# One table of places: the pieces of a two-layer graph attention kernel put in another order

## The chip, the cores and the metric

The kernel runs on one core of a Trainium2 chip. The metric is the device time of one execution in microseconds (us). Three executions of the kernel before took 2467.41, 2478.37 and 2482.59 us, so its median is 2478.37 us. The profile used here is of one more execution, whose span from the first to the last instruction is 2471.9 us, with a mean granted TensorE clock of 0.997. All data is fp32.

## The reference

There are 128 graphs of 128 nodes with 512 features, and one adjacency matrix for all. Two layers follow each other.

```python
# layer 0: scores weighted by the adjacency, divided by their norm, no softmax
q, k, v = x @ Wq.T, x @ Wk.T, x @ Wv.T
rel = adjacency.T * (q @ k.T)
rel = rel / norm(rel, axis=2)
x = layernorm(x + rel @ v)
# layer 1: attention with 8 heads of 64 features, masked where adj == 0
q, k, v = x @ Wq + bq, x @ Wk + bk, x @ Wv + bv
weights = softmax(q @ k.T / sqrt(64) + mask)        # per head
x = layernorm(x + weights @ v)
```

## The kernel before

**Rounds.** The 128 graphs are worked in 32 rounds of 4 graphs (`NG = 32`, `G = 4`). A round has five projections, called `m` (layer 0, query and key weights folded into one matrix), `v0`, `q`, `k` and `v1`. Each is done by a two-level scheme that replaces matrix products by sums. Its pieces are `inner` (line 458: two or four products of 128x128 by 128x128) and `whole` (line 503: two products of 128x128 by 128x256).

**Layer 0.** `l0_score` (line 544, four 128-column products of a graph), `l0_norm` (line 558: the column sums of the squares, as products of 32 columns of the array, tile `pn`), `l0_out` (line 594, one 512-column product), `l0_layernorm`.

**Layer 1, for each graph b = 0 to 3.** `attn_scores` (line 611) makes eight products, one for each head, that contract over 64 rows only (tile `ps`, line 617). VectorE adds the mask and finds the maxima (`masked`, line 129), 16 instructions a graph. `attn_exp` (line 633) is on ScalarE, two heads a piece. Then the weights are transposed with the help of DRAM: `attn_spill` (line 640) writes them out, `attn_stage` (line 646) reads them back in another arrangement into the tile `wl`, of which there is one, and `attn_transpose` (line 654) is one VectorE instruction over 128x1024 elements. `attn_out` (line 661) makes eight products that fill 64 columns of the array (tile `po`, line 669). `attn_back` and `attn_rows` send the result through DRAM again, `attn_res` fetches the residual, `attn_sum` adds (VectorE line 701, GpSimd lines 703 and 705), and `attn_stats`, `attn_norm` and `attn_write` finish the graph. The last round does its attention in another form (`last_...`).

**Weights.** Of each projection's weights a part stays on the chip and a part (896 KB) is fetched each round by `stream` (line 191) into a ring of two tiles named `wr`.

**What sets the order.** Nothing decides the order at run time. Every piece has a place in the table `KEYS` (line 814): five numbers, for round 0, for round 1, for the rounds 2 to 29, for round 30 and for the last round, counted in units of which 35 make a round (`R = 35`). All pieces are sorted by 35 x round + place, and each engine's queue is filled in that order:

```python
    def at(f, g, a, n):
        keys = KEYS[n]
        k = keys[0] if g is None else R * g + keys[0 if g == 0 else 1 if g == 1 else 4 if g == NG - 1 else 3 if g == NG - 2 else 2]
        todo.append((k, len(todo), f, a))
...
    with tc.manual_schedule():
        layer0_weights()
        for _, _, f, a in sorted(todo, key=lambda t: t[:2]):
            f(*a)
```

Each engine takes its own queue in order and waits at its head; SyncE (SP) issues all DMAs, in order too. A place above 35 means that the piece is done while later rounds are under way: graph 2's scores of a round, at 61.65, stand at 26.65 of the next round. Below, places are given within a round, modulo 35.

The short products are these two loops:

```python
        for a in range(H // 2):                      # attn_scores, line 614
            for s in range(2):
                r = slice(s * HD, (s + 1) * HD)
                nc.tensor.matmul(p[s][:, :, a, :], QT[g][r, a, b, :], KT[g][r, a, b, :], start=True, stop=True)
...
        for a in range(H // 2):                      # attn_out, line 666
            for s in range(2):
                h = 2 * a + s
                nc.tensor.matmul(p[s * HD:(s + 1) * HD, a, :], V1[g][b // 2][:, b % 2, h * HD:(h + 1) * HD],
                                 wT[:, s * (H // 2) + a].rearrange("p q t -> p (q t)"), start=True, stop=True)
```

PSUM tiles come from two pools: `ps_m` with six banks (line 53; the scores of a graph take two, the results of `attn_out` one) and `ps_a` with two (line 52).

Of the kernel before, what the change touches and what calls it, by code (L numbers as in the profile page):

```python
# [18 lines left out]
def kernel(  # L19
# [786 lines left out]
    def last_store(g, b):  # L806
# [8 lines left out]
        ("inner", "k", 0, 0): (33.9, 26.7, 31.7, 34.3, 21.3),  # L815
        ("inner", "k", 0, 1): (34.7, 28.4, 34.6, 35.7, 22),
        ("inner", "k", 0, 2): (36, 30.6, 35.74, 37.9, 22.8),
        ("inner", "k", 0, 3): (39, 34.1, 37.5, 39.8, 23.9),
        ("inner", "k", 1, 0): (37, 27.9, 33.04, 35.6, 21.9),
        ("inner", "k", 1, 1): (38.2, 29.3, 33.9, 35.8, 22.7),  # L820
        ("inner", "k", 1, 2): (38.5, 30.7, 35.7, 38.8, 23),
        ("inner", "k", 1, 3): (39.8, 33.2, 37.1, 40, 24),
        ("inner", "m", 0, 0): (None, -48, -24.4, -25.1, -24.6),
        ("inner", "m", 0, 1): (None, -44, -22.46, -21.7, -23),
        ("inner", "m", 0, 2): (None, -40, -20.83, -20, -21.47),
        ("inner", "m", 0, 3): (None, -31.2, -19, -16.2, -19.8),
        ("inner", "m", 1, 0): (None, -43, -23, -23, -24.5),
        ("inner", "m", 1, 1): (None, -39.4, -21.8, -21.8, -21.8),
        ("inner", "m", 1, 2): (None, -32, -20.2, -20.3, -21),
        ("inner", "m", 1, 3): (None, -30, -18.3, -14.4, -18),  # L830
        ("inner", "q", 0, 0): (25.2, 32.3, 27.73, 27.2, 11.2),
        ("inner", "q", 0, 1): (28.7, 32.6, 28.24, 33.4, 13.2),
        ("inner", "q", 0, 2): (30.3, 37, 31.6, 35.46, 16),
        ("inner", "q", 0, 3): (32.3, 38, 32.6, 36, 25.3),
        ("inner", "q", 1, 0): (27.9, 34.7, 27.9, 27.7, 13),
        ("inner", "q", 1, 1): (29.5, 35.97, 29.31, 29.64, 15.97),
        ("inner", "q", 1, 2): (31, 37.7, 31, 31.7, 20.5),
        ("inner", "q", 1, 3): (32.1, 38.7, 32.3, 35.5, 26.3),
        ("inner", "v0", 0, 0): (None, -46, -14.9, -14.1, -16.2),
        ("inner", "v0", 0, 1): (None, -31.4, -13.2, -12.9, -13.2),  # L840
        ("inner", "v0", 0, 2): (None, -27, -12.2, -12.5, -11),
        ("inner", "v0", 0, 3): (None, -24.3, -12, -11.4, -10),
        ("inner", "v0", 1, 0): (None, -39, -14.6, -14.01, -13.8),
        ("inner", "v0", 1, 1): (None, -32.6, -13.07, -12.6, -12.7),
        ("inner", "v0", 1, 2): (None, -26, -12.11, -12, -10.9),
        ("inner", "v0", 1, 3): (None, -22, -11, -11.3, -10.5),
        ("inner", "v1", 0, 0): (38.7, 39.05, 38.4, 41.3, 44),
        ("inner", "v1", 0, 1): (40.4, 41.08, 40.4, 42.6, 46.4),
        ("inner", "v1", 0, 2): (43, 44.89, 41.8, 45.6, 47.8),
        ("inner", "v1", 0, 3): (46.68, 45.5, 44.04, 46.6, 52),  # L850
        ("inner", "v1", 1, 0): (39.7, 39.27, 40.7, 41.6, 45),
        ("inner", "v1", 1, 1): (40.8, 40, 41.9, 45, 49.7),
        ("inner", "v1", 1, 2): (44.2, 44.2, 43.1, 45.4, 58),
        ("inner", "v1", 1, 3): (46.5, 44.8, 43.8, 46.4, 61),
        ("step", "m", 1): (-96, None, None, None, None),
        ("step", "m", 2): (-74, None, None, None, None),
        ("step", "m", 3): (-64, None, None, None, None),
        ("step", "m", 4): (-44, None, None, None, None),
        ("step", "m", 5): (-75, None, None, None, None),
        ("step", "m", 6): (-71, None, None, None, None),  # L860
        ("step", "m", 7): (-63, None, None, None, None),
        ("step", "v0", 1): (-49, None, None, None, None),
        ("step", "v0", 2): (-27, None, None, None, None),
        ("step", "v0", 3): (-28, None, None, None, None),
        ("step", "v0", 4): (-21.3, None, None, None, None),
        ("step", "v0", 5): (-45, None, None, None, None),
        ("step", "v0", 6): (-40, None, None, None, None),
        ("step", "v0", 7): (-31, None, None, None, None),
        ("whole", "k", 1, 0): (38, 34, 35.8, 38.09, 23.8),
        ("whole", "k", 1, 1): (39.2, 35, 37.9, 40.05, 26.5),  # L870
        ("whole", "k", 6, 0): (40.6, 38.1, 40.6, 42.5, 30),
        ("whole", "k", 6, 1): (42, 40.9, 42.3, 44.1, 35),
        ("whole", "k", 7, 0): (44, 42, 43.4, 45.11, 35.6),
        ("whole", "k", 7, 1): (44.1, 43, 44, 45.3, 38),
        ("whole", "m", 1, 0): (None, -39.3, -19.76, -19, -21.4),
        ("whole", "m", 1, 1): (None, -28, -17.6, -14.2, -19),
        ("whole", "m", 6, 0): (None, -25.9, -16.4, -14, -17),
        ("whole", "m", 6, 1): (None, -23, -14, -11.63, -14),
        ("whole", "m", 7, 0): (None, -16.6, -12.8, -11, -12.9),
        ("whole", "m", 7, 1): (None, -13.2, -12.02, -10, -11.7),  # L880
        ("whole", "q", 1, 0): (31.1, 37.4, 33.2, 37, 18),
        ("whole", "q", 1, 1): (38.4, 39.1, 35.6, 38.4, 27.5),
        ("whole", "q", 6, 0): (41, 39.8, 37.6, 39.82, 33),
        ("whole", "q", 6, 1): (42.7, 41.3, 40, 41, 35.5),
        ("whole", "q", 7, 0): (44.5, 44.1, 42.6, 44, 41),
        ("whole", "q", 7, 1): (45, 44.5, 43.2, 45.1, 42.3),
        ("whole", "v0", 1, 0): (None, -24, -10.3, -10.5, -9.99),
        ("whole", "v0", 1, 1): (None, -18, -9.66, -9.8, -9.5),
        ("whole", "v0", 6, 0): (None, -16, -8.9, -8.6, -8),
        ("whole", "v0", 6, 1): (None, -14, -7.28, -7.4, -7.7),  # L890
        ("whole", "v0", 7, 0): (None, -13.14, -6.58, -6.5, -5.4),
        ("whole", "v0", 7, 1): (None, -8, -5.68, -4.06, -5.37),
        ("whole", "v1", 1, 0): (46.7, 46.5, 44.05, 46.7, 56.6),
        ("whole", "v1", 1, 1): (47.7, 48.5, 46.2, 46.9, 60),
        ("whole", "v1", 6, 0): (49, 50.7, 47.6, 49.2, 64.4),
        ("whole", "v1", 6, 1): (50.2, 52.8, 49.4, 51.9, 67.2),
        ("whole", "v1", 7, 0): (50.85, 54, 52.56, 54, 72),
        ("whole", "v1", 7, 1): (53, 54.6, 53.4, 56, 73),
        ("attn_back", 0): (69.5, 67, 68.7, 83.7, None),
        ("attn_back", 1): (64.37, 65.6, 67.94, 92, None),  # L900
        ("attn_back", 2): (74.25, 76, 78.3, 97, None),
        ("attn_back", 3): (82.2, 83.6, 80.2, 63, None),
# [269 lines left out]
```

## Time and profile before

| what | us | share of the span |
|---|---|---|
| TensorE (PE) busy | 2421.0 | 98% |
| VectorE (DVE) busy | 1969.6 | 80% |
| GpSimd (POOL) busy | 1464.7 | 59% |
| ScalarE (ACT) busy | 1031.8 | 42% |
| DMA queue of SP: 549.81 MB | | 77.3% of 16 engines |

Over four rounds in the middle (1223 to 1533 us) the busy times change little from round to round: PE 76.6, 75.2, 76.6 and 75.9 us of 77 or 78 us, and VectorE 61 to 62 us of them. The share of PE is of modelled ends: a matmul's record is longer than the distance to the next one's start (a 128-column product of two records takes 0.223 us from start to start, while each record is 0.275 us long). So the starts are read here and not the lengths.

### The profile page before, as it was taken

The page shows a single profiled execution, that of the slowest core. Times are in us where ns is not written, and L with a number is a line of the kernel's source. Part 1 is how long each engine was busy: PE and PEld are TensorE (multiplying, and loading weights), DVE is VectorE, ACT ScalarE, POOL GpSimd, SP SyncE. Part 2 cuts the span into 40 slices and gives each one's busy share as a digit, 9 for nine tenths or more (in the row PEclk, how much of TensorE's full clock was granted, in tenths as well). Part 3 has the DMA queues.
Part 4 walks back from the last instruction along what each step waited for, and adds up shares of the span by engine and source line. Part 5 has one row for each costly group of instructions (what it writes and reads, how often), then busy time and mean ns, then how long its engine had stood idle before and what let it go on. Part 6 is the DMA issues. An engine that isn't in the chain of part 4 may idle for free.

```text
span 2471.9 us, 54459 instructions
## 1 busy us (share of the span) xinstructions
PE 2421.0 (98%) x18456; PEld 2147.3 (87%) x18456; DVE 1969.6 (80%) x5440; ACT 1031.8 (42%) x3598; POOL 1464.7 (59%) x1958
## 2 busy tenths in 40 slices
PE   8999999999999999999999999999999999999998
PEld 6889888889888888888898888888888988888887
DVE  5678888778888788787887877888887888877887
ACT  1244343444443443434434444444344344344354
POOL 5746655556565566555665555656556656556664
PEclk9999999999999999999999999999999999999999
DMA  8577877878787878778787788887787878787774
GB/s 203 175 200 223 249 221 221 240 211 244 225 229 227 222 226 237 221 221 231 233 244 212 223 232 227 228 235 232 218 232 229 250 220 228 224 233 222 241 224 140
DMA packets 532247, 553.28 MB, mean 224 GB/s; under 512 B 40192, under 2 KB 427392, under 8 KB 531968
## 3 DMA queue, kind: packets, MB, share of 16 engines
q1 hardware_dynamic: 531968, 549.81, 77.3%
q8 instruction: 145, 2.38, 0.4%
q14 instruction: 134, 1.10, 0.2%
HBM read 380.44 MB, written 169.21 MB: 222 GB/s over the span
## 4 chain that ended last, share of the span: by engine, by line
PE 72%; DMA 13%; DVE 5%; SPq 4%; POOL 3%; issue 2%; ACT 0%; DVEq 0%; POOLq 0%
PE pa_v L446 11%; PE pc_v L456 9%; PE pc_q L456 7%; DMA wl<-wd 7%; PE pc_k L456 5%; PE pa_k L446 5%; PE pa_q L446 5%; PE ps L617 4%; PE po L669 4%; PE pa_m L446 4%; PE po L597 4%; PE pc_m L456 4%; PE pst L552 3%; DMA wd<-w 3%; DMA xl_h<-x1d 2%
## 5 line engine op out<-in xcount | busy, mean ns | idle before, releaser
L637 ACT ACTIVATE w<-w,nmax 128x128 f32<-128x128 f32 x992 | 387.3, 396 | 308.6 <-DVE nmax L130 308.5
L446 PE MATMUL pa_v<-wc_v,tx 128*128 128x256 f32 x1024 | 264.6, 386 | 9.3 <-DVE v L501 9.0
L130 DVE CUSTOM_DVE_ANT_0 w<-ps,mask 128x128 f32<-128x128 f32 x1024 | 224.0, 286 | 44.0 <-PE ps L617 42.6
L446 PEld LDWEIGHTS pa_v<-wc_v,tx 128*128 128x128 f32 x1024 | 180.1, 191 | 35.0 <-DVE v L501 13.7
L637 ACT ACTIVATION_READ_ACCUMULATOR w<-w,nmax 128x1 f32 x992 | 191.1, 193 | 0.0
L656 DVE STREAM_TRANSPOSE wT<-wl 128x1024 f32<-128x1024 f32 x124 | 153.1, 1235 | 42.9 <-DMA wl<-wd 42.0
L567 POOL TENSOR_TENSOR rn<-ss,mhalf 128x4 f32<-128x4 f32 x32 | 33.0, 1031 | 207.6 <-DVE ss L565 207.6
L456 PE MATMUL pc_v<-wd_v,ux 128*128 128x128 f32 x756 | 146.3, 275 | 0.1
L456 PE MATMUL pc_v<-wr_v,tx 128*128 128x128 f32 x756 | 146.2, 275 | 0.0
L456 PE MATMUL pc_v<-wr_v,ux 128*128 128x128 f32 x756 | 146.2, 275 | 0.0
L701 DVE TENSOR_TENSOR o<-o,rs 128x512 f32<-128x512 f32 x118 | 126.4, 1075 | 23.3 <-DMA o<-od 23.2
L617 PEld LDWEIGHTS ps<-kT,qT 64*128 64x128 f32 x1984 | 118.2, 187 | 30.1 <-issue 19.9
L669 PE MATMUL po<-wT,v 128*64 128x128 f32 x1984 | 135.7, 279 | 7.1 <-DVE wT L656 6.8
L577 POOL TENSOR_SCALAR ve<-st 128x1 f32<-128x1 f32 (+1 forms) x157 | 35.8, 228 | 177.5 <-DVE st L573 169.6
L617 PE MATMUL ps<-kT,qT 64*128 64x128 f32 x1984 | 136.5, 282 | 0.0
L446 PE MATMUL pa_k<-tx,wc_k 128*128 128x256 f32 x512 | 134.2, 386 | 0.3 <-DVE kT L493 0.3
L446 PE MATMUL pa_q<-tx,wc_q 128*128 128x256 f32 x512 | 134.3, 385 | 0.1
L446 PE MATMUL pa_m<-tx,wc_m 128*128 128x256 f32 x512 | 131.4, 380 | 0.0
L669 PEld LDWEIGHTS po<-wT,v 128*64 128x64 f32 x1984 | 106.1, 136 | 29.1 <-issue 14.2
L456 PEld LDWEIGHTS pc_v<-wd_v,ux 128*128 128x128 f32 x756 | 124.3, 191 | 7.4 <-ACT s_v L475 0.5
L552 PEld LDWEIGHTS pst<-yT,xT 128*128 128x128 f32 x1024 | 125.0, 193 | 3.3
L597 PE MATMUL po<-v,rel 128*128 128x512 f32 x256 | 125.6, 594 | 0.0
(315 smaller groups left out, 7456.5 us busy)
## 6 DMA issues: line engine op xcount, KB each, us to landing
wd<-w SPq DMA_DIRECT2D x248, 256.0 KB, 3.6
wl<-wd SPq DMA_DIRECT2D x496, 128.0 KB, 3.9
wr_v<-wr_v SPq DMA_DIRECT2D x63, 896.0 KB, 6.9
xl_x<-in_x_dram SPq DMA_DIRECT2D x256, 128.0 KB, 3.6
x<-in_x_dram SPq DMA_DIRECT2D x64, 512.0 KB, 5.1
x1d<-x SPq DMA_DIRECT2D x64, 512.0 KB, 7.8
xl_h<-x1d SPq DMA_DIRECT2D x256, 128.0 KB, 5.0
od<-oT SPq DMA_DIRECT2D x496, 64.0 KB, 2.2
```

Source lines behind the costliest of these rows:

```text
L130: nc.vector.tensor_tensor_reduce(out=dst, in0=scores, in1=m, scale=-HD ** -0.5, scalar=3.0e38, op0=ALU.add, op1=ALU.min, accum_out=least)
L446: nc.tensor.matmul(bank[:, m, :], l[:, k, m * P:(m + 1) * P], r[:, k, :], start=start and m == 0 and k == 0, stop=(m == 1 and k == 1), ski ...
L456: nc.tensor.matmul(dst[:, n, :], l, r, start=start and n == 0, stop=True, skip_group_check=True)
L552: nc.tensor.matmul(p, XT[g][:, dc, b, :], YT[g][:, dc, b, :], start=(dc == 0), stop=(dc == C - 1))
L567: nc.gpsimd.tensor_tensor(RN[g], ss[:, :, 0], mhalf, op=ALU.pow)
L577: nc.gpsimd.tensor_scalar(ve[:, :n], stats[:, :n, 1], EPS, None, op0=ALU.add)
L597: nc.tensor.matmul(p, REL[g][0][:, b, :], V0[g][b // 2][:, b % 2, :], start=True, stop=True)
L617: nc.tensor.matmul(p[s][:, :, a, :], QT[g][r, a, b, :], KT[g][r, a, b, :], start=True, stop=True)
L637: nc.scalar.activation(w[:, s, :, a, :], w[:, s, :, a, :], AF.Exp, bias=nmax[:, i:i + 1], scale=-1.0, accum_out=sums[:, i:i + 1])
L656: nc.vector.transpose(wT, SOFT[g, b][0].rearrange("p a i r -> p i a r"))
L669: nc.tensor.matmul(p[s * HD:(s + 1) * HD, a, :], V1[g][b // 2][:, b % 2, h * HD:(h + 1) * HD], wT[:, s * (H // 2) + a].rearrange("p q t -> ...
L701: nc.vector.tensor_tensor(f, f, rs.rearrange("p s y a -> p (s y a)")[:, :, None].to_broadcast([P, A * H // 2, Q]), op=ALU.mult)
```

## The change

Only the numbers of `KEYS` change, nearly all of them. No instruction is added or removed and no tile changes its size: TensorE has 9243 matmuls before and after, VectorE 5440 instructions, SP 2448 DMAs. What moves is the order in each queue. The change is for two things: to bring the short attention products together, so that they stand in four blocks a round, and to put pieces that wait for a transfer later on, behind other work. The lines that matter below, for the rounds 2 to 29 the third number of each:

```diff
-        ("attn_scores", 0): (45.8, 44.9, 44.6, 46.702, None),
-        ("attn_scores", 1): (48.4, 45, 46.8, 49.5, None),
-        ("attn_scores", 2): (61, 61.5, 61.65, 53.3, None),
-        ("attn_scores", 3): (61.4, 62, 62.1, 46, None),
-        ("attn_out", 0): (65.1, 65.3, 65, 77.5, None),
-        ("attn_out", 1): (63, 63.4, 63, 64, None),
-        ("attn_out", 2): (73.3, 74.4, 74, 94, None),
-        ("attn_out", 3): (79.3, 80, 77.2, 58.4, None),
-        ("l0_norm",): (-19, -3, -4.5, -4.1, -5.3),
-        ("attn_exp", 1, 4): (50.8, 49.2, 48.25, 52, None),
-        ("attn_exp", 3, 6): (67, 66.4, 66.2, 46.99, None),
-        ("attn_spill", 1, 1): (51.3, 52.7, 55.2, 56.1, None),
-        ("attn_spill", 3, 1): (70.5, 68.4, 68.8, 49.8, None),
-        ("attn_stage", 0): (53.2, 53, 55.3, 62, None),
-        ("attn_stage", 1): (57.9, 59.2, 58.4, 60.8, None),
-        ("attn_stage", 2): (71, 71, 69.7, 82, None),
-        ("attn_stage", 3): (73.5, 76.5, 72.97, 51.8, None),
-        ("attn_transpose", 0): (56.9, 56.9, 57, 72, None),
-        ("attn_transpose", 1): (60.3, 60.5, 60.08, 61.4, None),
-        ("attn_transpose", 2): (71.9, 71.2, 72.05, 84, None),
-        ("attn_transpose", 3): (74.2, 78.9, 75.1, 56.6, None),
-        ("stream", "q"): (22, 28.2, 22.57, 26, 8.7),
-        ("stream", "v1"): (37.2, 37.9, 34.3, 37.1, 28.3),
+        ("attn_scores", 0): (46.611, 46.4, 45.8, 47.6, None),
+        ("attn_scores", 1): (46.8, 46.5, 45.9, 49, None),
+        ("attn_scores", 2): (61.6, 61.8, 62, 49.5, None),
+        ("attn_scores", 3): (62, 62, 62.7, 47.67, None),
+        ("attn_out", 0): (61.2, 66, 66, 86, None),
+        ("attn_out", 1): (67.1, 65.6, 61.8, 69.3, None),
+        ("attn_out", 2): (72.6, 74.33, 74.1, 104, None),
+        ("attn_out", 3): (82, 79.2, 80.72, 69, None),
+        ("l0_norm",): (-23, -3, -4.46, -4.2, -4.2),
+        ("attn_exp", 1, 4): (48.2, 51.7, 53.4, 55, None),
+        ("attn_exp", 3, 6): (69.1, 67, 68.9, 48.8, None),
+        ("attn_spill", 1, 1): (53, 53.8, 54.5, 62, None),
+        ("attn_spill", 3, 1): (71, 70.6, 71.2, 57, None),
+        ("attn_stage", 0): (57, 56.2, 55.9, 73, None),
+        ("attn_stage", 1): (61.1, 64.07, 58.6, 64, None),
+        ("attn_stage", 2): (67, 71, 71.4, 94, None),
+        ("attn_stage", 3): (74, 75.7, 76.72, 59.3, None),
+        ("attn_transpose", 0): (59.8, 60.07, 58.3, 76, None),
+        ("attn_transpose", 1): (63.8, 65.2, 60.8, 68.5, None),
+        ("attn_transpose", 2): (69.7, 71.2, 72.5, 95.1, None),
+        ("attn_transpose", 3): (75.81, 76.7, 76.74, 59.4, None),
+        ("stream", "q"): (17, 23, 24.12, 20.95, 9.5),
+        ("stream", "v1"): (33.8, 35.7, 39.3, 41, 36),
...
```

## The prediction

> **What bounds the kernel now.** I read the page's busy times and chain first, then the chain of waits of TensorE, then the order of its matmuls in time.
>
> ```profile
> span 2471.9 us, 54459 instructions
> ...
> PE 2421.0 (98%) x18456; PEld 2147.3 (87%) x18456; DVE 1969.6 (80%) x5440; ACT 1031.8 (42%) x3598; POOL 1464.7 (59%) x1958
> ...
> PE 72%; DMA 13%; DVE 5%; SPq 4%; POOL 3%; issue 2%; ACT 0%; DVEq 0%; POOLq 0%
> ```
>
> TensorE is the bound, with no engine near it; the DMA share of the chain says that transfers set some ends too. The waits of TensorE in the whole run:
>
> ```profile
> PE pc_m L456 <- DVE yT L480: 12.2, 22, 0.9
> PE pa_v L446 <- DVE v L501: 9.5, 15, 1.5
> PE po L669 <- DVE wT L656: 6.8, 8, 2.2
> PE pb_m L446 <- DVE wr_m L196: 4.3, 1, 4.3
> PE pc_q L456 <- POOL ux L309: 3.3, 1, 3.3
> ```
>
> These and the smaller ones sum to 43 us; in the rounds 2 to 29 (154 to 2345 us) they are 26 us, 0.9 us a round. Better waiting alone can therefore gain about 1%. What VectorE waited for tells where they come from:
>
> ```profile
> DVE wT L656 <- DMA wl<-wd: 42.0, 41, 3.8
> ...
> DVE o L701 <- DMA o<-od: 23.2, 19, 3.2
> ```
>
> Both are transfers at the head of its in-order queue; what stands behind them on VectorE (the additions for `yT` and `v`) then comes late for TensorE. The rest must be in the matmul stream itself. Its timeline around one graph's scores alone, two graphs' scores together, and `po` beside `pn`:
>
> ```profile
> 1258.43 1.03 PE L446 MATMUL pa_v<-wc_v,x1T 128*128 128x256 f32 x4
> 1259.39 1.16 PE L617 MATMUL ps<-kT,qT 64*128 64x128 f32 x16
> 1260.48 0.49 PE L456 MATMUL pc_m<-xT,wc_m 128*128 128x128 f32 x2
> 1260.81 0.39 PE L456 MATMUL pc_m<-tx,wr_m 128*128 128x128 f32 x2
> ...
> 1291.01 2.06 PE L617 MATMUL ps<-kT,qT 64*128 64x128 f32 x32
> 1292.99 1.13 PE L446 MATMUL pa_v<-wc_v,tx 128*128 128x256 f32 x4
> 1293.96 0.38 PE L456 MATMUL pc_q<-x1T,wc_q 128*128 128x128 f32 x2
> ...
> 1300.57 1.09 PE L669 MATMUL po<-wT,v 128*64 128x128 f32 x16
> 1301.60 0.43 PE L563 MATMUL pn<-sq,ones 128*32 128x128 f32 x8
> 1301.95 0.49 PE L456 MATMUL pc_q<-ux,wd_q 128*128 128x128 f32 x2
> 1302.28 0.39 PE L456 MATMUL pc_q<-tx,wr_q 128*128 128x128 f32 x2
> ```
>
> The first column is the start. Full-array products follow each other at 0.223 us (128 columns), 0.432 (256) and 0.859 (512). Four starts of `pa_v` at 0.216 end at 1259.29, but `ps` starts at 1259.39; and the first `pc_m` pair behind it takes 0.33 instead of 0.223. From 1259.29 to 1260.59, where the stream is regular again, the eight scores cost 1.29 us. The sixteen in one piece: 0.09 in front, 1.98, and 0.97 instead of 0.864 behind, 2.18 us. So a second graph in the same block costs 0.896 us, and opening and closing a block costs 1.29 - 0.896 = 0.39. A block of `po` alone has 1.22 us by the same reading, the two of `pn` alone (at 53.0 and 99.2 us) 0.55, and both together 1.58: 0.19 less than apart. Each change of the array's shape (128x128, 64 rows, 64 columns, 32 columns) thus costs 0.195 us, two a block, three where two kinds adjoin.
>
> **What the Trainium skill says.** "TensorEngine Tiling (Array Packing)", Key Properties: changing the tiling mode, not just the tile, drains the TensorE. The trace agrees: 0.09 us ahead of each new shape. "TensorE: Matmul & The Clock Gate", LDWEIGHTS: loading takes columns / 1.2 ns, 107 ns for 128; the extra 104 ns of the first pair behind a block looks like one such load with nothing to hide it. "Perfetto Trace Analysis", Identifying the Most-Contended Engine: matmul busy time is a poor measure of distance to the limit; here too, since 98% busy hides the block costs.
>
> **The change part by part.**
>
> *Blocks.* Before, a middle round has seven blocks by the places: out 2; out 3; scores 0; scores 1; scores 2+3; out 1; out 0 + `l0_norm`. Changes of shape: 6 x 2 + 3 = 15. After: out 3 (10.72) + scores 0 (10.8) + scores 1 (10.9); out 1 (26.8) + scores 2 + 3; `l0_norm` + out 0; out 2. That is 3 + 3 + 3 + 2 = 11. Four fewer save 4 x 0.195 = 0.78 us a round. Counting along the whole queue of both built kernels, first and last rounds too: 223 blocks with 478 changes before, 131 with 350 after. 128 x 0.195 = **25.0 us**, all on the bounding engine.
>
> Check of the price: 5000 products of 128 columns x 0.2234 + 1952 x 0.432 + 144 x 0.859 + 1024 scores x 0.112 + 992 outs x 0.104 + 9 us of small ones + 478 x 0.195 = 2404 us; with 58 us of gaps that I find in the stream (waits, the slow clock at the start) and 9 us before the first and after the last matmul this is 2471, the span.
>
> *A full PSUM.* A block of out + two scores takes five of the six `ps_m` banks, and then 32 VectorE instructions of 0.105 us must free four. Behind the second block q's first two `inner` want four banks at once. Before, scores 2+3 were followed by the same after one `whole` (0.87 us), and no wait of TensorE names line 130. Lining up VectorE's durations behind the places leaves about 0.4 us there: I take 0, at most 0.3 us a round.
>
> *Weight transfers.* `wr_q` takes the tile that v0's last piece frees (place 25.0); from there to its first use (27.91) are 8.7 us of matmuls, against 7.9 from issue to landing. Before, that transfer was issued from a tile free for 10 us. SP stands still until 25.0, so the queue ahead has drained; I take 0, with 0.5 us a round as the bad end. For `wr_v` of v1 the distance falls from 10.8 to 9.3 us, landing 6.9: nothing.
>
> *Pieces behind transfers.* Here the work between two places, in matmul time (`inner` 0.89 or 0.45, `whole` 0.87). Transposition 2 to 3, one `wl` for both: 5.6 before, 8.2 after. Needed: the transposition 1.2, four issues of 0.43, landing 3.9, so 6.8: too short before, enough now. Transposition 0 to 1: 6.2 before, 7.1 after, needed again 6.8. Against these: from the last exponential that stage 2 stands behind (spill 3,1 is ahead of it on SP) to transposition 2, 11.4 before and 6.2 after; needed 1.0 for the exponentials, 0.5 + 1.7 of issues, 3.9 landing: 7.1. But stream v1, 896 KB, no longer stands between. The same at transposition 0: 10.6 before, 7.9 after, needed 7.1. VectorE runs up to about 1 us behind the places, which helps. Behind a late transposition stand the additions that TensorE waits for, and out 1 now comes 0.8 us after its transposition is done (7.4 before). Sum: two places gain 1 to 2 us of room, two lose 3 to 5. VectorE's waits for transfers, 65 us or 2 us a round, I take as unchanged; TensorE's share 0.9 us a round, between 0.4 and 1.8.
>
> All other moves (exponentials, loads, writes, norms) have 9 us or more to their users or lie on engines that idle 20 to 58%; at nothing.
>
> Sum: 2478.4 - 25.0 + 0 = 2453.
>
> **The rivals.** (1) The likeliest, 0.52: the block costs go and waits stay, 2453 +/- 10; half of it is over 1%. (2) 0.22: longer rooms at transpositions 1 and 3 also halve the 26 us of waits: 2440. For it: 42 of 65 us of VectorE's transfer waits are `wl`. (3) 0.14: transpositions 0 and 2 wait longer, 0.8 us a round reaches TensorE, 31 x 0.8 = 25: 2478, no change. For it: 6.2 against 7.1 us. (4) 0.12, slower: late transfers pile up on SP, whose queue is in order; with 2.5 us a round, 31 x 2.5 - 25 = +52: 2530. Against: DMA is busy 77%, as before, and VectorE idles 15 us a round in which it catches up.
>
> **How the numbers follow.** Over 1% faster means below 2453.6: half of (1) and all of (2), 0.48. Within 1%: the rest of (1) and (3), 0.40. Slower: 0.12. The range from 2432 to 2494 leaves out most of (4) and the far end of (2).
>
> **What would show it.** Right: blocks of 16 + 32 records of `po` and `ps` of 3.2 us, four a round; PE's busy sum little changed and a middle round 0.8 us shorter; waits of TensorE still near 26 us. Wrong: more than 2 us a round of VectorE's waits for `wl` or `o`, TensorE waits on `wT`, on line 130 or on `wr_q`; or a change of shape between `po` and `ps` that costs more than the 0.195 us read beside full products.

## The result and the profile after

The changed kernel took 2408.48 us (median of 4, 2407.43 to 2412.64), the kernel before beside it 2477.74 (2467.41 to 2482.59): a ratio of 0.9729, 95% interval 0.9696 to 0.9762. The forecast was 2453 with a range down to 2432, so the gain is 69 us where 25 were forecast. In what follows one run of g3 (2688.30 us), taken in a slower state of the chip, is left out of the median.

The page of the changed kernel, for the three lines shown of before:

```profile
span 2410.9 us, 54547 instructions
...
PE 2387.0 (99%) x18456; PEld 2150.6 (89%) x18456; DVE 1963.5 (81%) x5440; ACT 1021.1 (42%) x3598; POOL 1449.8 (60%) x1958
...
PE 93%; DMA 4%; DVE 2%; POOL 1%; ACT 0%; issue 0%; SPq 0%; POOLq 0%; DVEq 0%; ACTq 0%
```

The work is the same to a per cent or two on every engine (the 88 instructions more are of the sequencers, which wait and issue); the chain is not. Transfers and SP's queue had 13% and 4% of it and now have 4% and 0%, TensorE 93% instead of 72%. The waits of TensorE (line waited for, us in total, times, longest):

```profile
PE pb_m L446 <- DVE wr_m L196: 3.6, 1, 3.6
PE po L669 <- DVE wT L656: 3.5, 4, 1.3
PE pc_m L456 <- POOL tx L279: 1.6, 1, 1.6
```

The two that led before, `pc_m` for `yT` (12.2 us) and `pa_v` for `v` (9.5 us), are gone from the top. The waits of VectorE, with many lines left out:

```profile
DVE v L501 <- PE pa_v L446: 105.4, 119, 2.2
...
DVE wT L656 <- DMA wl<-wd: 8.4, 8, 2.1
...
DVE o L701 <- DMA o<-od: 0.5, 1, 0.5
```

The two transfer waits fell from 42.0 and 23.2 us to 8.4 and 0.5. VectorE now waits for TensorE, as it should beside an engine that is the bound. And TensorE's timeline around a block of out 1 with the scores of two graphs:

```profile
1260.81 1.03 PE L446 MATMUL pa_v<-wc_v,tx 128*128 128x256 f32 x4
1261.77 1.09 PE L669 MATMUL po<-wT,v 128*64 128x128 f32 x16
1262.79 2.06 PE L617 MATMUL ps<-kT,qT 64*128 64x128 f32 x32
1264.78 0.49 PE L456 MATMUL pc_q<-x1T,wc_q 128*128 128x128 f32 x2
```

Read as in the prediction, `po` and 32 records of `ps` in one block cost 3.204 us (median of 56 blocks), against 1.219 + 2.180 = 3.40 us for the two apart: 0.195 less, one change of shape saved.

Where the 61 us between the two profiled spans went, from the starts of TensorE's matmuls:

| part | before | after | difference |
|---|---|---|---|
| blocks of short products at their price | | | -25 |
| gaps over 0.12 us in the stream | 57.8 | 24.9 | -33 |
| smaller gaps and the two ends | | | -3 |

A gap is the time from the start of one matmul to the next beyond the regular distance. In the rounds 2 to 29 (154 to 2345 us of the kernel before) the gaps are 35.4 us before and 4.8 after. Giving each gap to a wait of VectorE for a transfer (over 0.15 us) that lies up to 9 us ahead of it, the 35.4 us divide so: 8.7 behind transposition 1, 6.4 behind transposition 2, 3.0 behind transposition 3, 16.8 behind sum 3, and 0.5 behind none. After: 4.1 behind transposition 1 and 0.6 behind none. That is a division by nearness in time, of one execution of each kernel; f1 and g1 below test it. One of the sum's cases in the kernel before, VectorE's timeline first and TensorE's after it (start, duration; in brackets the idle time ahead and what ended it):

```profile
1346.18 1.41 DVE L701 TENSOR_TENSOR o<-o,rs 128x512 f32<-128x512 f32 x1 [1.77 <-DMA o<-od]
1347.52 0.68 DVE L480 TENSOR_TENSOR yT<-pc_m,yT 128x512 f32<-128x512 f32 x1
```

```profile
1348.25 0.49 PE L456 MATMUL pc_m<-ux,wc_m 128*128 128x128 f32 x2 [0.56 <-DVE yT L480]
...
1349.78 0.49 PE L456 MATMUL pc_m<-ux,wc_m 128*128 128x128 f32 x2 [0.81 <-DVE yT L480]
```

Sum 3 stands 1.77 us for `o`; the addition for `yT` behind it, which waits for no transfer itself, comes late, and TensorE stops twice. The named reason on TensorE is `yT`; the cause is one place further.

### The profile page after: what moved, and what is told of

Same layout as the page of the kernel before. It is cut to its first block, busy times and chain, and to the rows that moved or that the text cites. A ratio compares the mean times of both kernels' runs of the same rounds, so it can differ in the third digit from the quotient of the medians.

```text
span 2410.9 us, 54547 instructions
## 1 busy us (share of the span) xinstructions
PE 2387.0 (99%) x18456; PEld 2150.6 (89%) x18456; DVE 1963.5 (81%) x5440; ACT 1021.1 (42%) x3598; POOL 1449.8 (60%) x1958
## 4 chain that ended last, share of the span: by engine, by line
PE 93%; DMA 4%; DVE 2%; POOL 1%; ACT 0%; issue 0%; SPq 0%; POOLq 0%; DVEq 0%; ACTq 0%
PE pc_v L456 13%; PE pa_v L446 13%; PE pc_q L456 8%; PE pc_k L456 7%; PE pa_q L446 7%; PE pa_k L446 7%; PE pc_m L456 7%; PE pa_m L446 6%; PE po L669 5%; PE ps L617 5%; PE po L597 4%; PE pst L552 4%; PE pd_v L456 2%; DMA wr_k<-wr_k 2%; PE pd_k L456 1%; PE pd_q L456 1%
## 5 line engine op out<-in xcount | busy, mean ns | idle before, releaser
L446 PE MATMUL pa_v<-wc_v,tx 128*128 128x256 f32 x1024 | 253.9, 380 | 1.6 <-DVE v L542 0.9
L446 PEld LDWEIGHTS pa_v<-wc_v,tx 128*128 128x128 f32 x1024 | 186.0, 190 | 23.5 <-DVE v L542 1.3
L705 POOL TENSOR_TENSOR xr<-xr,o 128x512 f32<-128x512 f32 x58 | 73.8, 1272 | 191.2 <-DVE o L701 99.3
L486 POOL TENSOR_TENSOR qT<-qT 128x512 f32<-128x512 f32 x32 | 40.7, 1273 | 183.8 <-ACT qT L484 183.2
L501 DVE TENSOR_TENSOR v<-pa_v,v 128x256 f32<-128x256 f32 x190 | 79.6, 419 | 80.0 <-PE pa_v L446 79.5
L493 DVE SCALAR_TENSOR_TENSOR qT<-pa_q,bq_sb,qT 128x256 f32<-128x256 f32 x256 | 112.2, 469 | 20.3 <-PE pa_q L446 17.4
L617 PE MATMUL ps<-kT,qT 64*128 64x128 f32 x1984 | 127.6, 278 | 0.0
L498 DVE TENSOR_TENSOR v<-pa_v,v 128x512 f32<-128x512 f32 x95 | 62.3, 684 | 79.5 <-PE pa_v L446 79.5
L446 PE MATMUL pa_k<-tx,wc_k 128*128 128x256 f32 x512 | 126.7, 380 | 0.0
```

The costliest lines, as they stand in the source:

```text
L446: nc.tensor.matmul(bank[:, m, :], l[:, k, m * P:(m + 1) * P], r[:, k, :], start=start and m == 0 and k == 0, stop=(m == 1 and k == 1), ski ...
L493: nc.vector.scalar_tensor_tensor(o, self.a[:, m], b1[self.kind][:, 2 * eh + m:2 * eh + m + 1], o, op0=ALU.add, op1=ALU.add)
L501: nc.vector.tensor_tensor(o[:, m], self.a[:, m], s[:, m], op=ALU.add)
L705: nc.gpsimd.tensor_tensor(xr_, xr_, o.rearrange("p (f a r) -> p f a r", f=A, a=H // 2), op=ALU.add)
```

## Experiments

Two theories at the start. First: blocks and waits are two separate gains, and the second comes from room, that is from putting the waiting piece later. Second: it comes from the transfers landing earlier, because something else stands ahead of them on SP. All edits are third numbers in the table (rounds 2 to 29). Times are medians; the kernel before beside them took 2471 to 2475 us. The ratio is not the quotient of the medians shown; it is estimated over the runs of both kernels. The gaps are those of one execution from 154 to 2345 us, which in the longer runs ends some rounds short of round 29.

| run | us | ratio to before (95%) | gaps from 154 to 2345 us |
|---|---|---|---|
| e2, after with 460 changes of shape | 2430.98 | 0.9833 (0.9806 to 0.9860) | 5.3 |
| e1, before, blocks alone | 2585.63 | 1.0460 (1.0433 to 1.0487) | 150.3 |
| e3, before, waits later alone | 2728.95 | 1.1038 (1.1009 to 1.1068) | 229.0 |
| e4, after, SP's queue put back | 2589.78 | 1.0479 (1.0455 to 1.0503) | 158.3 |
| f1, before, two streams behind stages | 2455.17 | 0.9913 (0.9882 to 0.9943) | 10.7 |
| f2, before, sum 3 and users later | 2480.13 | 1.0035 (1.0020 to 1.0050) | 34.0 |
| f3, before, blocks and users | 2482.49 | 1.0040 (1.0026 to 1.0054) | 52.9 |
| f4, f1 + f3 | 2453.72 | 0.9919 (0.9894 to 0.9943) | 26.7 |
| g1, f4 with sum 3 later | 2439.35 | 0.9867 (0.9847 to 0.9887) | 14.0 |
| g2, after, load and stream k moved | 2509.27 | 1.0153 (1.0127 to 1.0179) | 83.3 |
| g3, g2 + a larger block | 2650.42 | 1.0709 (1.0666 to 1.0752) | 185.9 |
| h1, after, load behind stage 1 | 2414.24 | 0.9759 (0.9726 to 0.9793) | 7.2 |
| h2, after, larger block and users | 2407.34 | 0.9732 (0.9702 to 0.9762) | 8.4 |
| i1, after, load behind stream q | 2405.77 | 0.9721 (0.9695 to 0.9748) | 1.3 |
| i2, h2 + i1 | 2404.11 | 0.9717 (0.9693 to 0.9742) | 8.0 |
| i3, after again | 2408.27 | 0.9729 (0.9706 to 0.9752) | 2.8 |

**The clock in five of them.** In e1, e3, e4, g2 and g3 the mean granted clock of the profiled execution was 0.960 to 0.985, against 0.997 in the kernel before and 0.995 in the changed one. In e4 TensorE stops 4.3 us ahead of an out 2, and the clock granted from 413.7 to 417 us is then 0.50:

```profile
413.88 1.98 PE L669 MATMUL po<-wT,v 128*64 128x128 f32 x16 [4.29 <-DVE wT L656]
```

At the full clock the same 16 records took 1.09 us. Of e4's 27 stops over 1.5 us (between 100 and 2400 us), 20 end in such a stretch of half the clock; the three of the kernel before, of 1.5 to 2.2 us, don't. From the starts of the matmuls inside these stretches, the half clock cost an estimated 50 us in e1, 75 in e3, 60 in e4, 30 in g2 and 85 in g3, and 3 in the kernels before and after. The losses of these five are thus larger than the waits themselves, and part of this stands in the column of gaps.

**The price of a change of shape (e2).** The changed kernel with two of its blocks taken apart, 350 changes to 460:

```diff
-        ("attn_scores", 1): (46.8, 46.5, 45.9, 49, None),
-        ("attn_out", 3): (82, 79.2, 80.72, 69, None),
-        ("attn_out", 1): (67.1, 65.6, 61.8, 69.3, None),
+        ("attn_scores", 1): (46.8, 46.5, 47.5, 49, None),
+        ("attn_out", 3): (82, 79.2, 79.99, 69, None),
+        ("attn_out", 1): (67.1, 65.6, 63.01, 69.3, None),
```

> The changed kernel with its blocks taken apart again in the rounds 2 to 29: scores 1 behind the next inner piece, out 3 ahead of v1's third inner piece, out 1 behind q's first two inner pieces. Changes of shape: 350 to 460. Theory 1: 110 x 0.195 = 21.5 us slower than the changed kernel, 2430 us, with VectorE's waits for wl still near 8 us. Theory 2: 40 us or more slower, and waits for wl and o come back.

2430.98 us, 22.5 more than the changed kernel; 110 x 0.195 = 21.5. The gaps stayed as they were (5.3 us). The price and the count hold.

**Blocks alone (e1).** The kernel before with the three pieces moved that make four blocks, nothing else:

```diff
-        ("attn_scores", 1): (48.4, 45, 46.8, 49.5, None),
-        ("attn_out", 3): (79.3, 80, 77.2, 58.4, None),
-        ("attn_out", 1): (63, 63.4, 63, 64, None),
+        ("attn_scores", 1): (48.4, 45, 44.61, 49.5, None),
+        ("attn_out", 3): (79.3, 80, 79.59, 58.4, None),
+        ("attn_out", 1): (63, 63.4, 61.64, 64, None),
```

> The kernel before with three places of the rounds 2 to 29 changed, so that its short products stand in the four blocks of the changed kernel: scores 1 right behind scores 0, out 3 right ahead of them, out 1 right ahead of scores 2. Changes of the array's shape: 478 to 367. Theory 1 (each change costs 0.195 us, and the rest of the gain comes from waits for transfers): 111 x 0.195 = 21.6 us faster, 2456 us, with VectorE's waits for wl and o and TensorE's waits near those of before (65 and 43 us). Theory 2 (the tighter blocks themselves bring VectorE into step and so remove the waits too): 50 us or more faster, below 2428 us. Theory 3 (blocks of out + two scores run into the six PSUM banks): less than 12 us faster, with TensorE waits on line 130.

114 us slower, though each of 54 blocks cost its 3.2 us. SP's waits, then VectorE's:

```profile
SPq L682 <- DVE rs L674: 135.9, 48, 4.7
```

```profile
DVE o L701 <- DMA o<-od: 117.6, 36, 6.6
```

Out 3 came later and what follows it did not: SP stood at back 3 (line 682; 35.6 us before), and sum 3 waited for `o` in 25 of 25 middle rounds. Of the 150 us of gaps, 135.9 lie behind sum 3, matmuls at half the clock included.

**Waits later alone (e3).** The kernel before with the four transpositions and sum 3 later, and their users left where they were:

```diff
-        ("attn_sum", 3): (88.2, 88.8, 83.8, 74.8, None),
-        ("attn_transpose", 0): (56.9, 56.9, 57, 72, None),
-        ("attn_transpose", 1): (60.3, 60.5, 60.08, 61.4, None),
-        ("attn_transpose", 2): (71.9, 71.2, 72.05, 84, None),
-        ("attn_transpose", 3): (74.2, 78.9, 75.1, 56.6, None),
+        ("attn_sum", 3): (88.2, 88.8, 87.6, 74.8, None),
+        ("attn_transpose", 0): (56.9, 56.9, 58.0, 72, None),
+        ("attn_transpose", 1): (60.3, 60.5, 61.2, 61.4, None),
+        ("attn_transpose", 2): (71.9, 71.2, 72.88, 84, None),
+        ("attn_transpose", 3): (74.2, 78.9, 76.85, 56.6, None),
```

> The kernel before with only VectorE's pieces that wait for a transfer put later in the rounds 2 to 29: transpositions 0, 1, 2 and 3 by 1.0, 1.1, 0.8 and 1.75 places, sum 3 by 3.8 places. Nothing of SyncE's queue and no block moves. Theory P (later places of the waiting pieces remove the waits): VectorE's waits for wl fall from 42 to below 15 us and for o from 23 to below 3, and the time falls by 20 to 33 us, to 2445 to 2458. Theory S (it is the order of SyncE's queue that brings the transfers in earlier): the waits fall by half at most, as each transfer starts later where it waits for a transposition, and the time by less than 12 us.

The transfer waits fell to 2.4 us (transpositions) and to none (sum 3), and the kernel lost 257 us. Its largest waits of VectorE at line 572 and of TensorE:

```profile
DVE bs L572 <- POOL xr L705: 104.4, 27, 3.9
```

```profile
PE pa_m L446 <- DVE yT L501: 105.8, 27, 4.0
```

Stats 3 now stood right behind sum 3 and waited for GpSimd's addition, with `yT` behind it; TensorE also waited 90.1 us for `wT` in out 2 and out 3. More room for one piece is taken from its user. Neither theory had this.

**SP's queue (e4, f1).** In e4 only SP's order changes. Stream v1 goes back ahead of stage 2 in the changed kernel (x1_stage 1 was moved along and made no difference that the trace shows):

```diff
-        ("attn_stage", 2): (67, 71, 71.4, 94, None),
-        ("stream", "v1"): (33.8, 35.7, 39.3, 41, 36),
-        ("x1_stage", 1): (3, 20.7, 8.14, 20, 9.4),
+        ("attn_stage", 2): (67, 71, 71.45, 94, None),
+        ("stream", "v1"): (33.8, 35.7, 36.44, 41, 36),
+        ("x1_stage", 1): (3, 20.7, 17.0, 20, 9.4),
```

> The changed kernel with two orders of SyncE's queue put back in the rounds 2 to 29: the weights of v1 (896 KB) ahead of stage 2 again, and the second half of the layer's staging (x1_stage 1, 512 KB) ahead of graph 0's spill again. Nothing of the other engines moves. Theory S: stages 0 and 2 land 2 to 5 us later, VectorE's waits for wl rise from 8 to above 30 us, and the time rises by 10 to 30 us, to 2418 to 2438. Theory P: the waits stay below 12 us and the time within 5 us of 2408.

181 us more than the changed kernel: the direction of the second theory, at many times its size. SP's waits, and TensorE's:

```profile
SPq L193 <- PE pc_q L456: 166.3, 31, 11.5
```

```profile
PE po L669 <- DVE wT L656: 123.5, 31, 6.3
```

In this order stream v1 must wait for the tile that q's last piece frees, SP stands there (45.8 us without the edit), and stage 2 behind it is issued 11.1 us after graph 2's last exponential instead of 5.1. Transposition 2 waits in 25 of 25 rounds, 157 us. TensorE's own wait for it is 123.5 us, and the estimated 60 us of half clock are about the rest of the 181.

f1 does the opposite on the kernel before: two transfers of 896 KB go right behind the stages that they stood ahead of.

```diff
-        ("stream", "q"): (22, 28.2, 22.57, 26, 8.7),
-        ("stream", "v1"): (37.2, 37.9, 34.3, 37.1, 28.3),
+        ("stream", "q"): (22, 28.2, 23.45, 26, 8.7),
+        ("stream", "v1"): (37.2, 37.9, 34.75, 37.1, 28.3),
```

> The kernel before with two places changed: the 896 KB transfers stream v1 and stream q go right behind the stages they stood ahead of (v1 34.3 to 34.75, behind stage 2 at 34.7; q 22.57 to 23.45, behind stage 1 at 23.4). In the trace of before TensorE's gaps that follow VectorE's wait at transposition 1, 2 and 3 are 8.7, 6.4 and 3.0 us in the rounds 2 to 29. Theory A (a big transfer ahead in SP's in-order queue, or beside the stage in the DMA engines, makes the stage late): these gaps go, all or most; transposition 2's 11 waits of 16.4 us and transposition 1's 14 of 12.8 us fall to less than half; 2472 - 10 to 18 = 2454 to 2462 us. Theory B (the stage is late because of what is ahead of the spills, not because of these two): waits unchanged, 2472 within 4 us.

16 us faster with two numbers. The waits at transpositions 1 and 2 fell from 12.8 and 16.4 us to none, and the gaps behind transpositions 1 to 3 from 18.1 to 0.7 us. Those behind sum 3 are halved too (16.8 to 8.8): `o` lands 0.9 us sooner after out 3. One stage 2 in the timeline of the kernel before, and one in f1 (start, duration of the issues):

```profile
1308.40 0.34 SPq L193 DMA_DIRECT2D wr_v<-wr_v  x1
1308.79 2.69 SPq L652 DMA_DIRECT2D wl<-wd  x4
...
1319.67 1.25 DVE L656 STREAM_TRANSPOSE wT<-wl 128x1024 f32<-128x1024 f32 x1 [2.87 <-DMA wl<-wd]
```

```profile
1288.86 1.94 SPq L652 DMA_DIRECT2D wl<-wd  x4
1290.90 0.38 SPq L193 DMA_DIRECT2D wr_v<-wr_v  x1
...
1297.71 1.23 DVE L656 STREAM_TRANSPOSE wT<-wl 128x1024 f32<-128x1024 f32 x1
```

Here SP doesn't stand: it issues stream v1 and goes on. But the last of the stage's 4 x 128 KB then lands 6.2 us after its issue (median of stage 2), and 4.7 us with v1 behind them. The Trainium skill, "DMA: Bandwidth & Descriptors", Queues, rings and completion order, says that SP has one ring on each of the 16 DMA engines and that descriptors are consumed in ring order; the trace fits that: 896 KB at 224 GB/s, the mean in the profile of the kernel before, is an estimated 4.1 us of the engines' time, of which the stage had to sit out what was left.

**The users moved along (f2, f3, f4, g1).** f2 puts sum 3 of the kernel before later, this time with stats 3 and norm 3:

```diff
-        ("attn_sum", 3): (88.2, 88.8, 83.8, 74.8, None),
-        ("attn_stats", 3): (92.7, 92.6, 87.7, 81, None),
-        ("attn_norm", 3): (93.6, 92.84, 91.72, 85, None),
+        ("attn_sum", 3): (88.2, 88.8, 87.55, 74.8, None),
+        ("attn_stats", 3): (92.7, 92.6, 90.45, 81, None),
+        ("attn_norm", 3): (93.6, 92.84, 93.2, 85, None),
```

> The kernel before with sum 3 put later (83.8 to 87.55) and its followers with it (stats 3 87.7 to 90.45, norm 3 91.72 to 93.2); blocks, back 3 and rows 3 as before. In before, 16.8 us of TensorE's gaps in the rounds 2 to 29 follow VectorE's wait at sum 3 for the DMA of o. Theory A (the room between a transfer and the piece that waits for it is what counts, if the piece's users move along): the waits o<-od go, 2472 - 14 to 17 = 2455 to 2458 us. Theory B (a piece that waits later only moves the stall on to the next user, as with transpositions whose users stayed): no gain or slower, 2472 to 2500 us, with waits of VectorE at stats 3 for GpSimd.

The waits for `o` went, and the time rose by 0.35%. In its place, VectorE's timeline and then TensorE's:

```profile
1275.76 0.69 DVE L572 BATCH_NORM_STATS2 bs<-xr 128x6 f32<-128x512 f32 x1 [0.72 <-POOL xr L705]
1276.49 0.18 DVE L573 BATCH_NORM_AGGREGATE st<-bs 128x2 f32<-128x6 f32 x1
1276.59 0.39 DVE L501 TENSOR_TENSOR yT<-pa_m,yT 128x256 f32<-128x256 f32 x1
```

```profile
1277.13 1.10 PE L446 MATMUL pa_m<-tx,wc_m 128*128 128x256 f32 x4 [0.19 <-POOL ve L577]
```

Stats 3 waits for GpSimd 0.72 us (18.7 us in 24 waits in all), the addition that frees the `pa_m` bank stands behind it, and TensorE starts some 0.36 us late in nearly every round. The releaser in the bracket is the last by the profile, and its 0.19 us is less than the gap; the order of VectorE's lines tells the rest.

f3 is e1 with the users of out 3 moved, f2's three and these two:

```diff
-        ("attn_back", 3): (82.2, 83.6, 80.2, 63, None),
-        ("attn_rows", 3): (83.6, 85, 83.4, 67, None),
+        ("attn_back", 3): (82.2, 83.6, 83.75, 63, None),
+        ("attn_rows", 3): (83.6, 85, 86.5, 67, None),
```

> The kernel before with four blocks a round (scores 1 46.8 to 44.61, out 3 77.2 to 79.59, out 1 63 to 61.64) and this time with what follows out 3 moved along: back 3 80.2 to 83.75, rows 3 83.4 to 86.5, sum 3 83.8 to 87.55, stats 3 87.7 to 90.45, norm 3 91.72 to 93.2. Theory A (the 114 us that the blocks alone lost were the wait at sum 3 for o and SP's stand at back 3): the waits o<-od go, the 111 changes of shape less give 21.6 us and the gaps behind sum 3 16.8 us: 2472 - 38 = 2434 us, 2428 to 2442. Theory B (the blocks cost something else, such as yT late behind 32 masks on VectorE): above 2460 us, with TensorE waiting for yT or v without a transfer wait of VectorE ahead.

Of e1's 114 us 103 came back, and the expected gain did not: the blocks cost 21.6 us less than before, but sum 3 still waits for `o` in 14 of 25 rounds, stats 3 for GpSimd (12.7 us), and transposition 1's share of the gaps is 14.0 us instead of 8.7. f4 is f3 with f1's two numbers:

> The kernel before with all of the last three: four blocks a round, the followers of out 3 later, streams v1 and q behind their stages; twelve numbers of the table. Theory A (block changes and rooms add up, and all else of the change does nothing): 2472 - 21.6 - 16.8 - (10 to 18) = 2416 to 2424 us, within 16 us of the changed kernel's 2408. Theory B (the changed kernel needs the whole reordering; single moves collide): above 2440 us.

2453.72 us, no better than f1 alone. (Ten numbers differ from the kernel before, not the twelve of the expectation.) Its transpositions wait no more (1.4 us in 25 rounds), and its 21.7 us saved on blocks went again into gaps around sum 3 and stats 3: 26.7 us in the middle rounds, and many under 0.12 us. g1 moves those once more, behind pieces of TensorE that need nothing of them:

```diff
-        ("attn_sum", 3): (88.2, 88.8, 87.55, 74.8, None),
-        ("attn_stats", 3): (92.7, 92.6, 90.45, 81, None),
-        ("attn_norm", 3): (93.6, 92.84, 93.2, 85, None),
+        ("attn_sum", 3): (88.2, 88.8, 88.65, 74.8, None),
+        ("attn_stats", 3): (92.7, 92.6, 91.97, 81, None),
+        ("attn_norm", 3): (93.6, 92.84, 94.2, 85, None),
```

> The last kernel (blocks, followers of out 3 moved, streams behind their stages: 2453.7 us) with sum 3 and its followers moved once more: sum 3 87.55 to 88.65 (behind the piece whole m 6, 0), stats 3 90.45 to 91.97, norm 3 93.2 to 94.2. There sum 3 still waited for o in 15 of 25 rounds, and 25 us of TensorE's gaps in the rounds 2 to 29 came with it or in the pieces of m and v0 around it. Theory A (sum 3 stands too near its transfer and ahead of additions that TensorE waits for): o<-od goes, gaps of the middle rounds fall from 27 to under 10 us, 2453.7 - 17 to 30 = 2424 to 2437 us. Theory B (VectorE has no room for 32 masks ahead of m's pieces in this order, wherever sum 3 stands): 2445 to 2455 us.

14.4 us less, 2 us short of the expected band; waits for `o` in the middle rounds and stats 3's waits for GpSimd are gone (0.8 us left). Ten pieces moved in the kernel before thus bring 32 us, about half of what the whole change brings (63 to 69 us, by which runs of the kernel before are taken). Not all of these edits put a wait later: since f3, rows 3 no longer stands right behind four loads of 128 KB, and its 256 KB land 2.7 us after their issue instead of 5.4. The two profiled spans, 2436.0 us and the changed kernel's 2410.9, differ by 25 us: 9 us of gaps in the middle rounds, 6 us in the rounds 0, 1, 30 and 31 whose numbers g1 leaves as they were, 17 changes of shape (3 us), and the rest in gaps under 0.12 us. That part is read from the traces and was not undone piece by piece.

**The last wait of the changed kernel (g2, h1, i1).** Transposition 1 still waits there. g2 takes stream k and a load of 512 KB from ahead of stage 1 to behind it:

```diff
-        ("stream", "k"): (19, 22.4, 21.9, 25.15, 13.9),
-        ("load_staged", 1): (None, -139, -47.5, -43.7, -42.9),
+        ("stream", "k"): (19, 22.4, 23.65, 25.15, 13.9),
+        ("load_staged", 1): (None, -139, -46.3, -43.7, -42.9),
```

> The changed kernel with stream k (21.9 to 23.65) and load_staged 1 (-47.5 to -46.3, which is 22.5 to 23.7 of the round) right behind stage 1 (23.6). In the changed kernel transposition 1 is the one that still waits (7 of 25 rounds, 8.1 us), and 4.1 us of TensorE's gaps follow it. Theory A (what stands ahead of a stage on SP makes it late): these go, 2408.5 - 4 = 2404.5 us. Theory B (the load or stream k is now late for its own user): 2408 to 2425 us, with TensorE or VectorE waiting for wr_k or xl_x.

No transposition waits any more, but the kernel is 101 us slower than the changed one, above either theory's range, and TensorE's waits begin with this line:

```profile
PE pc_q L456 <- DMA wr_q<-wr_q: 57.7, 22, 5.5
```

Stream q follows directly, and its median from issue to landing rose from 5.3 to 9.2 us. h1 moves the load alone (-47.5 to -46.3):

> The changed kernel with load_staged 1 alone put behind stage 1 (-47.5 to -46.3; stream k stays ahead at 21.9). Moving stream k with it had made TensorE wait for wr_q (75 us of gaps before the first product with wr_q, 22 named waits), while transposition 1 waited no more. Theory A (the load ahead of stage 1 is what makes transposition 1 late): its waits go, wr_q is in time, 2408.5 - 4 = 2404.5 us, 2402 to 2407. Theory B (it is stream k's 896 KB that makes stage 1 late): transposition 1 still waits in some 7 of 25 rounds, 2408.5 within 2 us. Theory C (load_staged 1 between stage 1 and stream q is enough to make wr_q late): above 2415 us, TensorE waiting for wr_q.

Transposition 1 waits no more, so it was the load; but `wr_q` lands in 6.7 us, TensorE waits for it in nine rounds (7.2 us of gaps), and the time is 6 us above the changed kernel's. Theories A and C each came true by half. i1 puts the load behind stream q (-47.5 to -45.85), so that neither stands behind it:

> The changed kernel with load_staged 1 put behind stream q (-47.5 to -45.85, which is 24.15 of the round), so that neither stage 1 nor stream q stands behind it on SP. Theory A (h1 freed transposition 1 and lost the same time again because the load stood between stage 1 and stream q): no wait at transposition 1, no wait for wr_q, 2408.5 - 4 = 2404.5 us, 2402 to 2407. Theory B (wr_q comes late because the load shares the DMA engines with it, wherever it stands on SP): TensorE still waits for wr_q, 2408 to 2415 us.

Both waits are gone, `wr_q` lands in 5.2 us, and the gaps of the middle rounds are 1.3 us, the least of all kernels. The median is 2.5 us under the changed kernel's on the same chip (i3); the runs overlap (2404.18 to 2407.93 against 2406.02 to 2408.70).

**A larger block (g3, h2, i2).** g3 is g2 with out 2 put into the block of out 3 and scores 0 and 1:

```diff
-        ("inner", "v1", 1, 3): (47, 45.7, 46, 46, 64),
-        ("attn_out", 2): (72.6, 74.33, 74.1, 104, None),
-        ("attn_back", 2): (75.83, 76.6, 79.9, 107, None),
+        ("inner", "v1", 1, 3): (47, 45.7, 45.705, 46, 64),
+        ("attn_out", 2): (72.6, 74.33, 80.71, 104, None),
+        ("attn_back", 2): (75.83, 76.6, 81.2, 107, None),
```

> The kernel g2 with out 2 put into the block of out 3 and scores 0 and 1 (74.1 to 80.71, its back 2 79.9 to 81.2, and inner v1 1, 3 from 46 to 45.705, ahead of the block): 294 changes of shape instead of 350. Theory A (the price holds): 56 x 0.195 = 10.9 us less, 2404.5 - 10.9 = 2393.6 us. Theory B (the block then wants all six ps_m banks and TensorE waits in it for VectorE to free them, some 0.4 to 1 us in each of 27 rounds): no gain, 2404 to 2425 us, with blocks of 32 + 32 records longer than 3204 + 1024 = 4.08 to 4.2 us.

The 27 blocks of 32 + 32 records cost 4.079 us each, without a wait for PSUM in them. But 141 us more than g2 were lost elsewhere. SP in its timeline (lines of other engines left out):

```profile
1340.01 1.20 SPq L89 DMA_DIRECT2D xl_h<-x1d  x2
...
1350.27 0.78 SPq L682 DMA_DIRECT2D od<-oT  x2
```

SP stands 9 us at back 2, and loads queued behind it come late: GpSimd waited 145 us for `xr` (line 703), TensorE 95 us for `yT`. h2 starts from the changed kernel and moves the users along:

```diff
-        ("attn_back", 2): (75.83, 76.6, 79.9, 107, None),
-        ("attn_rows", 2): (86.1, 81.8, 85.26, 114.5, None),
-        ("attn_sum", 2): (86.4, 83.7, 86.2, 126, None),
+        ("attn_back", 2): (75.83, 76.6, 84.82, 107, None),
+        ("attn_rows", 2): (86.1, 81.8, 87, 114.5, None),
+        ("attn_sum", 2): (86.4, 83.7, 88.81, 126, None),
```

> The changed kernel with out 2 in the block of out 3 and scores 0 and 1, as before (out 2 74.1 to 80.71, inner v1 1, 3 46 to 45.705), but with what follows out 2 moved along: back 2 79.9 to 84.82 (behind res 2), rows 2 85.26 to 87, sum 2 86.2 to 88.81 (behind whole v1 7, 0). In the first try the blocks had their price (4.08 us), but SP stood up to 9 us at back 2, and what is behind it there (loads of x, res 2) came late: VectorE and TensorE gaps of 185 us. Theory A (the followers were all of it): SP stands no more at back 2, 56 changes less, 2408.5 - 10.9 = 2397.6 us, 2394 to 2402. Theory B (32 masks and two oT on VectorE behind one block, or sum 2 so close to sum 3, make additions for m and v1 late): 2405 to 2440 us, with TensorE waiting for yT or v.

The losses are gone: 2407.34 us, only 1 us below the changed kernel and outside theory A's 2394 to 2402. The blocks cost 9 us less than in the changed kernel, and 4 us come back as gaps in a few rounds. i2 joins h2 and i1; i3 is the changed kernel beside them:

> Both: the block of out 2, out 3, scores 0 and 1 with its followers moved, and load_staged 1 behind stream q. From the two traces: the merged block gave 9 us on the blocks and cost 3 to 4 us in new gaps, the load is worth 4 to 5 us. Theory A (they add up): 2408.5 - 6 - 4.5 = 2398 us, 2395 to 2402. Theory B (the gain of either comes back as a wait of the other): 2404 us or more.

> The changed kernel once more, beside the two on one chip: 2408 us, 2405 to 2413, by all theories. The two versions are compared with this run.

i2 took 2404.11 us (2401.55 to 2408.30), i3 2408.27 (2406.02 to 2408.70). The medians differ by 4.2 us and the runs overlap, so that i2 beats the changed kernel is likely and not settled. 10 us were expected of it; its gaps over the whole run went up by 7 us against i3, 5.2 of them at products that wait for `wr_v`.

## Why the prediction was wrong, by its steps

**What bounds the kernel.** Right that TensorE does, and that what it waited for came from VectorE's waits for transfers. Too small in size: the named waits of TensorE in the rounds 2 to 29 gave 26 us, while the starts of its matmuls give 35.4 us of gaps, nearly all (34.9) behind a transfer wait of VectorE.

**Blocks.** Right: 3.204 us for a block of `po` and two scores, 128 changes less, 25 us. e2 measured 22.5 us for 110 changes. A change between `po` and `ps` costs what one beside a full product does. That 0.104 us of it is a weight load with nothing to hide it is not shown: the trace gives a load of 128 columns 0.19 us and one of 64 columns 0.136.

**A full PSUM, weight transfers, all the rest at nothing.** Right for the first two: no wait at line 130 of any size, and `wr_q` is in time. The margin at `wr_q` is thin, though: h1 shows 7 us of gaps from a load of 512 KB ahead of it, g2 75 us from that load and stream k. "All other moves at nothing" was wrong for sum 3, below.

**Pieces behind transfers: the step that failed.** The prediction said "VectorE's waits for transfers, 65 us or 2 us a round, I take as unchanged". They fell to 9 us, and with them 31 of the 35 us of gaps. The step compares, for each waiting piece, the room (until VectorE reaches it) with the need (until its transfer has landed). Measured from the prediction's own starting points, as medians of 25 middle rounds, in us:

| piece, measured from | room before, after | landed before, after |
|---|---|---|
| transposition 0, last exponential of graph 1 | 9.2, 7.9 | 9.0, 6.2 |
| transposition 1, start of transposition 0 | 7.9, 7.4 | 8.0, 6.8 |
| transposition 2, last exponential of graph 3 | 11.2, 7.4 | 11.0, 5.4 |
| transposition 3, start of transposition 2 | 6.6, 10.0 | 6.4, 7.5 |
| sum 3, last product of out 3 | 15.6, 15.9 | 16.3, 13.7 |

The rooms were counted within 2 us of this: 10.6 and 7.9 at transposition 0, 6.2 and 7.1 at 1, 11.4 and 6.2 at 2, 5.6 and 8.2 at 3. Only at transposition 1 was the sign of the change wrong. What failed is the need, and what was left out at sum 3.

First, the need was put at 6.8 to 7.1 us for both kernels, with one landing of 3.9 us, the median over all stages. Before, it was up to 11.0; after, 5.4 to 7.5. At transpositions 0 and 2 the room shrank by 1.3 and 3.8 us, and the need by 2.8 and 5.6. The prediction saw that stream v1 "no longer stands between" and gave it no number. f1 gives it: with v1 and q behind their stages the need at transposition 2 falls from 11.0 to 7.7 us and at transposition 1 from 8.0 to 5.5, for 16 us of time. e4 shows the same from the other side: with v1 back ahead, stage 2 of the changed kernel lands 13.5 us after graph 3's last exponential instead of 5.4. At transposition 0 no run took it apart. The traces show another 896 KB ahead: stream v0 is issued 0.7 us before graph 0's first spill in the kernel before, which then takes 7.5 us to land, and 6.6 us before it in the changed one, where it takes 2.6.

Second, the 23 us at `o` were counted in and not worked out, though out 3, back 3, rows 3, sum 3 and stats 3 all move. They set 16.8 us of the gaps, the largest single share. By their places sum 3 comes 6.6 behind out 3 before and 7.9 after, in units of the table, which looks like more room; in time it is 0.3 us more. But `o` lands 2.6 us sooner. Rows 3 is issued 1.0 us behind four loads of 128 KB before and lands in 5.4 us; after, these stand 12 us ahead, and it lands in 2.9. In the order of the kernel before, e1, f2, f3 and g1 show that three things count at sum 3: its room, the landing of rows 3, and what stands behind sum 3 and stats 3 on VectorE. In the changed kernel's own order it was not taken apart, so how the 16.8 us divide among these stays open.

So only at transposition 3, with 3.0 us of the gaps, did the wait go by a clearly later place, which was one aim of the change; elsewhere the transfers came sooner.

**The rivals.** The second (waits halve, 2440 us) had the right direction at about half of the size, but its reason, more room at transpositions 1 and 3, holds at 3 alone. The third and fourth had waits grow at transpositions 0 and 2; those stopped waiting altogether. The pile-up on SP that the fourth describes is real: e4 (+181 us) and g3 are such cases. The changed kernel is not one.

## To carry to other kernels

Where queues are in order, ask of each wait not only how far the waiting piece stands behind its transfer but what stands ahead of that transfer on the queue that issues it, and what stands behind the waiting piece on its own engine. Moving one piece is seldom a move: out 3 alone lost 114 us, and most of it came back when back, rows, sum and stats went along. A place in an order is no time; take distances between engines from the trace, with the landing time of that transfer in that order and not as a median over all transfers. And when an experiment loses much, look at its granted clock before the loss is put down to the wait alone.

## Not expected of the hardware

One transfer whose tile was not yet free, put ahead of four others, cost 181 us in e4, or 6.5 us in each of 28 rounds. About 4.4 us of that is TensorE's wait (123.5 us in all); a further 2, by the estimate above, come from the half clock in which most of the stops of some 4 us ended. In the stretch of the kernel before shown above, the four transfers of 128 KB issued just behind 896 KB landed 8.5 to 9.1 us after their issue, the next four of the same kind 3.9 to 4.0. And in the larger block 16 more records of `po` cost 0.875 us behind others of their kind against 1.219 alone, so joining like with like saved 0.344 us and not the 0.39 of two changes.
